# The first half product of a block as seven quarter products, worked in during the block before

## Chip, core and metric

The kernel runs on one core of one Trainium2 chip. The metric is the device time of one launch in microseconds (us); the time before is the median of three runs. Below, PE is TensorE, DVE is VectorE, ACT is ScalarE, POOL is GpSimd, SP is the engine that here only issues DMAs. "PEld" rows are PE's weight loads.

## What is computed

Input x is 32 images of 14 x 14 x 512 in fp32. Two layers follow. The first is by far the larger: a group norm, then 18 blocks, each a 512 x 512 product with bias and gelu. After blocks 1, 4 and 9 the activation is kept as an anchor; after blocks 11, 14 and 17 (the targets) a small network on the pooled activation makes gates, and a gated sum of the three anchors is added. The second layer is a group norm and a grouped 3 x 3 convolution. Cut to what matters here:

```python
for i in range(NUM_BLOCKS):
    nx = jax.nn.gelu(jnp.einsum('bhwc,cd->bhwd', x, block_w[i]) + block_b[i])
    if i in TARGET_IDX:
        ...
        nx = nx + gammas[t] * routed
    x = nx
    if i in ANCHOR_IDX:
        anchors.append(x)
```

## The kernel before

**Tiles.** The 32 images go in 8 pairs of tiles; a tile is two images, N = 392 pixels, with channels on the 128 partitions. A step is one block of one pair: a product of the 512 x 512 weights with 512 channels x 784 pixels, in fp32. There are 18 x 8 = 144 steps and one gap; `steps` (L99 to L110) lists them. Mostly runs of 3 or 6 blocks of one pair alternate with runs of the neighbouring pair.

**Seven half products.** A step would be eight half products (256 x 256 weights with 256 channels x 392 pixels), in a 2 x 2 scheme over channel halves and the two tiles. The kernel does Winograd's form of Strassen's scheme: seven half products on sums of weights (`sums`, s0 to s3, L398) and on sums of activations (`pre_adds`, t0 to t3, L440). The weight sums are worked out for the first pair and kept in DRAM (skeep); later pairs load them. One half product is 2 output halves d x 2 K halves = four matmuls of 128 x 128 weights with 392 columns (`part`, L480, does one d: two matmuls); an fp32 matmul leaves two records in the trace.

**One of the seven once more.** The product of s0 and t0 (accumulators Z) is itself done by seven quarter products, each one matmul with 196 columns (`inner`, L532). They need four weight sums u (`inner_sums`, L419) and four activation sums v (end of `pre_adds`, L453 to L460), and between them small copies of quarters of Z by ACT (L548, L549, L554, L563) and one add on DVE (L569, "the add of f").

**Order in a step** (`block`, L462; seven ticks, NP7 = 7, at which `run(tick)` lets out other work):

- X = a11 q00, each half copied to Y by ACT (`save`, L543)
- first quarter matmuls of Z; tick 0
- Y0 += a12 q10 with d = 0, two quarter matmuls of Z, Y1 += a12 q10 with d = 1; gelu of Y gives output quarter (0,0); tick 1
- X0 += s1 t1, copied to c2; two quarter matmuls of Z; tick 2
- X1 += s1 t1, copied to c2; the last quarter matmul of Z and the add of f; Z copied to c3; tick 3
- X += s2 t2; DVE adds X to c3; gelu gives quarter (1,1); tick 4
- Z += s3 q11; DVE adds Z to c2 (L523); gelu gives quarter (0,1); tick 5
- t0 and the four v of the next step on DVE (L586); X += a22 t3; gelu gives quarter (1,0); tick 6; then t1, t2, t3 of the next step (L592).

Here q00, q01, q10, q11 are the four quarters of the step's input (first index: channel half; second: tile), and X0, X1 the two accumulators of X. t0 is q01 - q00 of the next input, so that it needs both the gelu of Z and that of Y where the next step is of the same pair. Where the next step belongs to the other pair, its input has long been there.

Every engine works its instructions in the order of the program. PSUM has six banks for X, Y, Z and the convolution's sums (L79).

**Planner.** All other work (gates, norms, loads, building the convolution's weights, the convolution's units) is put into ticks by `put` (L130), against a budget of us for DVE and ACT in each tick (`ROOM`, L117). Weight loads (`load_block`, L386) come one step ahead (L1409), the sums' loads at ticks 3 to 5 (L1412), all on SP. The convolution's units (`plan_unit`, L1097) may stand at ticks 1 to 4 (`fits`, L1094).

Of the kernel before, what the change touches and what calls it, by code (L numbers as in the profile page):

```python
# [20 lines left out]
def kernel(  # L21
# [51 lines left out]
    qpool = ctx.enter_context(tc.tile_pool(name="qpool", bufs=38))  # L73
# [43 lines left out]
    ROOM = {"dve": (3.3, 1.9, 1.4, 1.8, 1.4, 0.6, 0.0), "act": (1.5, 0.75, 0.75, 0.8, 1.5, 1.5, 1.5)}  # L117
# [239 lines left out]
    def plan_start(p):  # L357

        t0 = NP7 * at_step[p, 0]
        parts = [(2 * p + n, c) for n in range(2) for c in range(NCK)]  # L360
        NIN = 3
        a = t0 - LEAD
        at(a - 30, copy_in, p)
        turned = []
        b = 0
        for j, (t, c) in enumerate(parts):
            at(t0 - LEAD - 6 if j < NIN else turned[j - NIN], load_blocks, t, c)
            turned.append(put(max(a, turned[j - NIN] + 4 if j >= NIN else 0), {"dve": 0.45 + c % NH * 0.15}, turn_blocks, t, c))
            a = turned[j]
        for j, (t, c) in enumerate(parts):  # L370
            b = max(b, put(turned[j // NH * NH + NH - 1], {"dve": 0.7}, stats_in, t, c))
        b = put(b + 1, {"dve": 0.8}, lambda: whole(scales_mean(pst[p])))
        b = put(b + 1, {"dve": 0.2}, lambda: whole(scales_rstd(pst[p])))
        b = put(b + 2, {"dve": 0.8}, lambda: scales_newton(pst[p]))
        e = b
        for c in range(NCK):
            e = max(e, put(b, {"dve": 1.6}, norm_in, p, c))
        b = e

        assert b < t0 - 1  # L380
        at(t0 - 2, take_start, p)
# [3 lines left out]

    def load_block(k):  # L386
        w = wpool.tile([P, NCK, C], F32, tag="w", name=f"w_{k}")
        nc.sync.dma_start(w, block_w[steps[k][1]].rearrange("(k p) d -> p k d", p=P))
        D = C // 2
        wts[k] = dict(  # L390
            a11=w[:, :NH, :D], a12=w[:, NH:, :D], a21=w[:, :NH, D:], a22=w[:, NH:, D:], s={}
        )
# [24 lines left out]
    ukeep = [tc.dram_tile([P, 4 * P], F32, name=f"ukeep{i}") for i in range(NB)]  # L417

    def inner_sums(k):  # L419

        p, i = steps[k]
        d = wts[k]
        u = d["u"] = spool.tile([P, 4, P], F32, tag="u", name=f"u_{k}")
        if p > 0:
            nc.sync.dma_start(u.rearrange("p j d -> p (j d)"), ukeep[i])
            return
        a = corners(d["s"][0], P)
        for j, (i0, i1) in enumerate((  # L430
            (a[1][0], a[0][0]), (a[1][1], u[:, 0]), (a[1][1], a[1][0]), (a[0][1], u[:, 1]),
        )):
            nc.vector.tensor_tensor(u[:, j], i0, i1, ALU.subtract)  # L433
        nc.sync.dma_start(ukeep[i], u.rearrange("p j d -> p (j d)"))
# [5 lines left out]
    def pre_adds(p, q, name, js):  # L440


        t = ts.setdefault(p, {})
        for j in js:
            t[j] = quarter(f"t{j}_{name}")
            i0, i1 = [
                lambda: (q[0][1], q[0][0]),
                lambda: (q[1][1], t[0]),
                lambda: (q[1][1], q[0][1]),
                lambda: (q[1][0], t[1]),  # L450
            ][j]()
            nc.vector.tensor_tensor(t[j], i0, i1, ALU.subtract)  # L452
            if j == 0:  # L453
                v = t["v"] = quarter(f"v_{name}").rearrange("p k (n x) -> p (k n) x", x=HW)
                b = corners(t[0], HW)
                for l, (i0, i1, op) in enumerate((
                    (b[1][0], b[1][1], ALU.add), (v[:, 0], b[0][0], ALU.subtract),
                    (b[0][0], b[1][0], ALU.subtract), (b[0][1], v[:, 1], ALU.subtract),
                )):
                    nc.vector.tensor_tensor(v[:, l], i0, i1, op)  # L460

    def block(k):  # L462
# [17 lines left out]
        def part(acc, d, lhsT, rhs, first=False):  # L480
            for kk in range(NH):
                nc.tensor.matmul(  # L482
                    acc[d][:, :N], lhsT=lhsT[:, kk, d * P : (d + 1) * P],
                    rhs=rhs[:, kk, :], start=first and kk == 0, stop=kk == NH - 1,
                    skip_group_check=True,
                )
# [5 lines left out]
        def gelu(half, n, srcs):  # L492
            o = quarter(f"o{half}{n}_{name}")
            dst[half][n] = o
            for d in range(NH):
# [17 lines left out]

        def temps(j):
            return [tmp.tile([P, N], F32, tag="c", name=f"c{j}{d}_{name}") for d in range(NH)]
# [8 lines left out]


        a, b, u, v = corners(s[0], P), corners(t[0], HW), w["u"], t["v"]
        Z = []

        def corner(d, n):
            return Z[d][:, n * HW : (n + 1) * HW]  # L530

        def inner(d, n, lhsT, rhs, first=False):  # L532
            nc.tensor.matmul(  # L533
                corner(d, n), lhsT=lhsT, rhs=rhs, start=first, stop=True, skip_group_check=True
            )

        X = bank("x")
        Y = bank("y")  # L540
        for d in range(NH):
            part(X, d, w["a11"], q[0][0], True)
            save(Y, X, (d,))  # L543
        Z += bank("z")
        inner(1, 0, u[:, 0], v[:, 0], True)
        inner(1, 1, a[0][0], b[0][0])
        f = tmp.tile([P, N], F32, tag="c", name=f"f_{name}")[:, :HW]
        nc.scalar.copy(f, corner(1, 0))  # L548
        nc.scalar.copy(corner(0, 0), corner(1, 1))  # L549
        run(tick)  # L550
        part(Y, 0, w["a12"], q[1][0])
        inner(0, 0, a[0][1], b[0][1])
        inner(1, 1, u[:, 1], v[:, 1])
        nc.scalar.copy(corner(1, 0), corner(1, 1))  # L554
        part(Y, 1, w["a12"], q[1][0])
        gelu(0, 0, [Y[d][:, :N] for d in range(NH)])
        run(tick + 1)
# [3 lines left out]
        inner(1, 0, a[1][1], v[:, 3])  # L561
        inner(1, 1, u[:, 2], v[:, 2])
        nc.scalar.copy(corner(0, 1), corner(1, 1))  # L563
        run(tick + 2)
        part(X, 1, s[1], t[1])
        save(c2, X, (1,))
        inner(0, 1, u[:, 3], b[1][1])
        both = Z[1][:, :N].rearrange("p (n x) -> p n x", n=2)
        nc.vector.tensor_tensor(  # L569
            both, both, f.unsqueeze(1).to_broadcast([P, 2, HW]), ALU.add  # L570
        )
        c3 = temps(3)
        save(c3, Z)
        run(tick + 3)
        product(X, s[2], t[2])
        add(c3, X)
        gelu(1, 1, c3)
        run(tick + 4)
        product(Z, s[3], q[1][1])
        add(c2, Z)  # L580
        gelu(0, 1, c2)
        run(tick + 5)
        pn = steps[k + 1][0] if k + 1 < len(steps) and steps[k + 1][1] != GAP else None
        if pn is not None:
            qn = dst if pn == p else cur[pn]
            pre_adds(pn, qn, f"{k + 1}", (0,))  # L586
        product(X, w["a22"], t[3])
        gelu(1, 0, [X[d][:, :N] for d in range(NH)])
        cur[p] = dst
        run(tick + 6)  # L590
        if pn is not None:
            pre_adds(pn, qn, f"{k + 1}", (1, 2, 3))  # L592
# [9 lines left out]
    def load_gates(k):  # L602
        ti = TARGETS.index(steps[k][1])
        w1 = fpool.tile([P, NCK, HID], F32, tag="w1", name=f"w1_{k}")
        nc.sync.dma_start(w1, fc1_w[ti].rearrange("(k p) h -> p k h", p=P))
        w2 = fpool.tile([HID, NA * C], F32, tag="w2", name=f"w2_{k}")
        if steps[k][0] == 0:
            nc.sync.dma_start(w2, fc2_w[ti])
        else:
            nc.sync.dma_start(w2[:, C:], w2keep[ti])  # L610
        fcw[k] = w1, w2
# [3 lines left out]
    def gate_differences(k, t):  # L615


        w2 = fcw[k][1]
        for a in range(1, NA):
            nc.vector.tensor_tensor(  # L620
                w2[:, a * C : (a + 1) * C], w2[:, a * C : (a + 1) * C], w2[:, :C], ALU.subtract
            )
        nc.sync.dma_start(w2keep[t], w2[:, C:])
# [7 lines left out]
    def gate_hidden(k, t, name, box):  # L631
        w1, _ = fcw[k]
# [14 lines left out]
    def gate_logits(k, name, box):  # L647
        _, w2 = fcw.pop(k)
        h = box["h"]
        lps = box["l"] = aux(f"lps_{name}")  # L650
        for m in range(NCK, NL):
            nc.tensor.matmul(  # L652
                lps[:, m * NB4 : (m + 1) * NB4], lhsT=w2[:, m * P : (m + 1) * P], rhs=h,
# [440 lines left out]
    def fits(tick):  # L1094
        return steps[tick // NP7][1] == GAP or 1 <= tick % NP7 <= 4

    def plan_unit(m, u, tk, ahead, stay=False):  # L1097
# [12 lines left out]
        assert b // NP7 == a // NP7  # L1110
# [283 lines left out]
    pre_adds(0, cur[0], "0", range(4))  # L1394
    inner_sums(0)
    for j in range(2, 4):
        sums(0, j)

# [3 lines left out]
    for k in range(len(steps)):  # L1402
# [5 lines left out]
        if k > 0:  # L1408
            at(NP7 * (k - 1), load_block, k)  # L1409
            if p > 0:  # L1410
                at(NP7 * (k - 1) + 3, inner_sums, k)
            for tk, j in ((3, 0), (3, 1), (4, 2), (5, 3)):  # L1412
                at(NP7 * (k - 1) + tk, sums, k, j)
            if p == 0:
                at(NP7 * (k - 1) + 4, inner_sums, k)
                for tk, us in ((3, 0.5), (4, 0.0), (5, 0.0)):
                    left["dve"][NP7 * (k - 1) + tk] = us
        if i in TARGETS:
            at(NP7 * (k - 1 if k == len(steps) - 1 else k) + 4, load_gates, k)
            for tk, us in enumerate((1.2, 0.0, 0.3, 0.8, 0.3, 0.2, 0.0)):  # L1420
# [5 lines left out]
    for p in range(NPAIR):  # L1426
        plan_differences(p)
        for i in TARGETS[:-1]:
            a = plan_gates(p, i, plan_head(p, i), [[0, 1], [2, 3]])
            assert a < NP7 * at_step[p, i + 1] - 1, (p, i, a, NP7 * at_step[p, i + 1])  # L1430
# [54 lines left out]
```

## Time and profile before

| | |
|---|---|
| median of three runs | 2910.55 us (2909.18 to 2910.66) |
| the profiled execution | 2908.12 us |
| its span, first to last instruction | 2906.4 us, 33728 instructions |
| mean granted PE clock | 0.994 |
| PE matmul records of line L482 (392 columns) | 48 in each step |
| PE matmul records of line L533 (196 columns) | 14 in each step |
| L533 matmul z<-v,u: busy, mean of one | 215.0 us, 331 ns |
| L482 matmul x<-t,s: busy, mean of one | 833.3 us, 494 ns |
| L460, the v: mean of one | 354 to 362 ns |
| L569, the add of f: mean of one | 572 ns |
| L548, L549, L554, L563, the small copies: mean of one | 323, 328, 307, 307 ns |
| L519, copy of a whole accumulator: mean of one | 469 to 497 ns |
| DMA | 507.35 MB, mean 175 GB/s |

How to read it: matmuls are pipelined, and the length of a record holds the way through the array; so the mean of one is longer than the distance between two in a stream. A row of the timeline gives the start, the time from the first start to the last end, engine, line, operation, output and input, shape and count; in brackets the idle time before it and what ended it. A row of the groups also gives the idle time in front of all its instructions.

### The profile page before, as it was taken

The page shows a single profiled execution, that of the slowest core. Times are in us where ns is not written, and L with a number is a line of the kernel's source. Part 1 is how long each engine was busy: PE and PEld are TensorE (multiplying, and loading weights), DVE is VectorE, ACT ScalarE, POOL GpSimd, SP SyncE. Part 2 cuts the span into 40 slices and gives each one's busy share as a digit, 9 for nine tenths or more (in the row PEclk, how much of TensorE's full clock was granted, in tenths as well). Part 3 has the DMA queues.
Part 4 walks back from the last instruction along what each step waited for, and adds up shares of the span by engine and source line. Part 5 has one row for each costly group of instructions (what it writes and reads, how often), then busy time and mean ns, then how long its engine had stood idle before and what let it go on. Part 6 is the DMA issues. An engine that isn't in the chain of part 4 may idle for free.

```text
span 2906.4 us, 33728 instructions
## 1 busy us (share of the span) xinstructions
PE 2867.1 (99%) x10545; PEld 1889.0 (65%) x10545; DVE 1932.9 (67%) x3996; ACT 1548.5 (53%) x3865; POOL 78.7 (3%) x59
## 2 busy tenths in 40 slices
PE   8999999999999999999999999999999999999987
PEld 5666666666666666666666666666666666666667
DVE  6888878765487565774657746676466764655775
ACT  4445555555556454564545645555455554655551
POOL 0000000000000000000000000000000000000000
PEclk9999999999999999999999999999999999999999
DMA  5544566644575566664666656756567753453676
GB/s 190 181 156 160 177 198 190 187 148 158 160 196 154 164 192 175 200 171 141 209 178 179 179 162 180 202 173 187 160 183 202 183 165 130 136 174 120 195 223 162
DMA packets 494053, 507.35 MB, mean 175 GB/s; under 512 B 242915, under 2 KB 303922, under 8 KB 493874
## 3 DMA queue, kind: packets, MB, share of 16 engines
q1 hardware_dynamic: 478378, 487.12, 56.1%
q0 software_dynamic: 4608, 12.85, 2.4%
q10 hardware_dynamic: 10888, 5.22, 0.7%
q8 instruction: 85, 1.39, 0.2%
q14 instruction: 94, 0.77, 0.1%
HBM read 421.32 MB, written 94.99 MB: 178 GB/s over the span
## 4 chain that ended last, share of the span: by engine, by line
PE 94%; DMA 3%; DVE 2%; ACT 0%; SPq 0%; issue 0%; DVEq 0%; ACTq 0%
PE x L482 51%; PE y L482 13%; PE z L482 13%; PE z L533 11%; PE cps L1013 4%; PE lps L652 1%; DMA x<-x2d 1%; DMA xkeep<-xt 1%; PE hps L635 1%; DMA w<-in_L_conv_fc_w_dram 0%; DMA s<-skeep 0%; DVE x L1002 0%; DMA xin<-in_x_dram 0%; DMA bq<-band 0%; DVE t L452 0%
## 5 line engine op out<-in xcount | busy, mean ns | idle before, releaser
L482 PE MATMUL x<-t,s 128*128 128x392 f32 x2304 | 833.3, 494 | 0.3 <-ACT c L519 0.3
L482 PEld LDWEIGHTS x<-t,s 128*128 128x128 f32 x2304 | 427.5, 190 | 230.3 <-ACT c L519 0.9
L499 ACT ACTIVATE o<-c,bias 128x392 f32<-128x392 f32 x480 | 291.8, 619 | 352.9 <-DVE c L523 352.9
L482 PE MATMUL x<-t,w 128*128 128x392 f32 x1152 | 403.2, 493 | 0.0
L482 PE MATMUL y<-o,w 128*128 128x392 f32 x1088 | 402.6, 492 | 0.0
L482 PE MATMUL x<-o,w 128*128 128x392 f32 x1088 | 380.8, 493 | 0.0
L482 PE MATMUL z<-o,s 128*128 128x392 f32 x1088 | 380.8, 493 | 0.0
L523 DVE TENSOR_TENSOR c<-x,c 128x392 f32<-128x392 f32 x288 | 160.7, 565 | 265.8 <-PE x L482 192.8
L482 PEld LDWEIGHTS x<-t,w 128*128 128x128 f32 x1152 | 218.4, 190 | 158.7
L482 PEld LDWEIGHTS z<-o,s 128*128 128x128 f32 x1088 | 206.3, 190 | 149.7
L482 PEld LDWEIGHTS x<-o,w 128*128 128x128 f32 x1088 | 206.2, 190 | 149.5
L519 ACT COPY c<-x 128x392 f32<-128x392 f32 x288 | 140.0, 486 | 299.9 <-PE x L482 299.9
L452 DVE TENSOR_TENSOR t<-o,o 128x784 f32<-128x784 f32 x272 | 263.9, 970 | 51.1 <-ACT o L499 49.0
L569 DVE TENSOR_TENSOR z<-z,f 128x392 f32<-128x392 f32 x144 | 82.3, 572 | 314.1 <-ACT z L563 313.9
L452 DVE TENSOR_TENSOR t<-o,t 128x784 f32<-128x784 f32 x272 | 262.9, 966 | 0.8 <-PE x L482 0.7
L482 PEld LDWEIGHTS y<-o,w 128*128 128x128 f32 x1088 | 200.1, 190 | 75.9 <-ACT y L519 0.2
L523 DVE TENSOR_TENSOR c<-z,c 128x392 f32<-128x392 f32 x288 | 161.5, 563 | 111.5 <-PE z L482 110.9
L519 ACT COPY y<-x 128x392 f32<-128x392 f32 x288 | 133.6, 469 | 175.0 <-PE x L482 173.7
L533 PE MATMUL z<-v,u 128*128 128x196 f32 x864 | 215.0, 331 | 7.8 <-DVE u L433 4.5
L533 PEld LDWEIGHTS z<-v,u 128*128 128x128 f32 x864 | 157.1, 191 | 49.6 <-issue 10.6
L499 ACT ACTIVATE o<-x,bias 128x392 f32<-128x392 f32 x240 | 137.6, 582 | 63.6 <-PE x L482 55.7
L499 ACT ACTIVATE o<-y,bias 128x392 f32<-128x392 f32 x240 | 141.4, 590 | 53.1 <-PE y L482 53.1
(139 smaller groups left out, 3181.6 us busy)
## 6 DMA issues: line engine op xcount, KB each, us to landing
w<-in_L_conv_block_w_dram SPq DMA_DIRECT2D x144, 1024.0 KB
s<-skeep SPq DMA_DIRECT2D x504, 256.0 KB
u<-ukeep SPq DMA_DIRECT2D x126, 256.0 KB
x2d<-xc SPq DMA_DIRECT2D x116, 224.0 KB
x<-x2d SPq DMA_DIRECT2D x104, 224.0 KB
skeep<-s SPq DMA_DIRECT2D x72, 256.0 KB
xkeep<-xt SPq DMA_DIRECT2D x32, 392.0 KB
o<-xkeep POOLq DMA_DIRECT2D x32, 392.0 KB, 8.1
```

What stands on the lines that cost most here:

```text
L452: nc.vector.tensor_tensor(t[j], i0, i1, ALU.subtract)
L482: nc.tensor.matmul(acc[d][:, :N], lhsT=lhsT[:, kk, d * P : (d + 1) * P], rhs=rhs[:, kk, :], start=first and kk == 0, stop=kk == NH - 1, sk ...
L499: nc.scalar.activation(o[:, d, :], srcs[d], AF.Gelu_apprx_tanh, bias=bias[:, r : r + 1])
L519: nc.scalar.copy(cs[d][:, :N], acc[d][:, :N])
L523: nc.vector.tensor_tensor(cs[d], acc[d][:, :N], cs[d], ALU.add)
L533: nc.tensor.matmul(corner(d, n), lhsT=lhsT, rhs=rhs, start=first, stop=True, skip_group_check=True)
L569: nc.vector.tensor_tensor(both, both, f.unsqueeze(1).to_broadcast([P, 2, HW]), ALU.add)
L635: nc.tensor.matmul(hps[:, :NB4], lhsT=w1[:, kk, :], rhs=box["pooled"][:, kk, :], start=(kk == 0), stop=(kk == NCK - 1),)
L652: nc.tensor.matmul(lps[:, m * NB4 : (m + 1) * NB4], lhsT=w2[:, m * P : (m + 1) * P], rhs=h, start=True, stop=True,)
L1013: nc.tensor.matmul(pv[:, :, lo:hi], lhsT=bw[:, g, dy], rhs=xv[:, :, lo + dy - 1 : hi + dy - 1], start=g == 0 and j == 0, stop=j == 2, skip ...
```

## The change

- `ahead(k)` says for which steps the first product X is done in the step before: pairs other than the first, not block 0, not the block after a target, and one step left out.
- For these, X is done by seven quarter products (the same scheme as Z, now a class `Inner` in four parts), with their own weight sums u1 of a11 and their own v of q00. The u1 are worked out by DVE in the first pair's steps and kept in DRAM; later they are loaded into the place of a21 in the weight tile, which isn't needed there.
- Its parts stand among the half products of the step before: part 0 after s2 t2, part 1 within s3 q11, part 2 before a22 t3, part 3 within it. Then ACT copies the new X to the new Y.
- In every step, ahead or not: Y comes in one piece after X (or first of all), by K halves; Z's quarter products start after it; s2 t2 stands half before and half after Z's last quarter product; t0 and the v of the next step are queued in the tick before a22 t3 rather than after.
- Weights come in two or three DMAs for all pairs but the first, one tick earlier; the sums' loads move by one tick; the budgets `ROOM` are new, with more where the next step isn't ahead; the convolution's units may stand at ticks 0 and 1 only; the start does t0, then u, then t1, two weight sums, t2 and t3; the first third of the gate weights has its own tile.

The core of the diff:

```diff
-    ROOM = {"dve": (3.3, 1.9, 1.4, 1.8, 1.4, 0.6, 0.0), "act": (1.5, 0.75, 0.75, 0.8, 1.5, 1.5, 1.5)}
+    ROOM = {"dve": (2.1, 0.8, 2.2, 2.6, 0.5, 0.0, 0.0), "act": (0.4, 0.6, 1.0, 1.5, 0.75, 0.0, 1.5)}
...
+    def ahead(k):
...
+        p, i = steps[k]
+        if (p, i) == (NPAIR - 2, TARGETS[1] + 2):
+            return False
+        return p > 0 and i not in (GAP, 0) and i - 1 not in TARGETS
...
+            nc.sync.dma_start(a11, src[:, :NH, :D])
+            if ahead(k):
+                nc.sync.dma_start(a21, ukeep[i][1].rearrange("p (k d) -> p k d", k=NH))
+            nc.sync.dma_start(w[:, NH:], src[:, NH:])
...
+        def part(self, j):
+            a, b, u, v, at = self.a, self.b, self.u, self.v, self.corner
+            if j == 0:
+                self.mm(1, 0, u[0], v[:, 0], True)
+                self.mm(1, 1, a[0][0], b[0][0])
+                nc.scalar.copy(at(0, 0), at(1, 1))
+                self.f = tmp.tile([P, N], F32, tag="c", name=f"f_{self.name}")[:, :HW]
+                nc.scalar.copy(self.f, at(1, 0))
+            elif j == 1:
+                self.mm(0, 0, a[0][1], b[0][1])
+                self.mm(1, 1, u[1], v[:, 1])
+                nc.scalar.copy(at(1, 0), at(1, 1))
+            elif j == 2:
+                self.mm(1, 0, a[1][1], v[:, 3])
+                self.mm(1, 1, u[2], v[:, 2])
+                nc.scalar.copy(at(0, 1), at(1, 1))
+            else:
+                self.mm(0, 1, u[3], b[1][1])
+                both = self.acc[1][:, :N].rearrange("p (n x) -> p n x", n=2)
+                nc.vector.tensor_tensor(
+                    both, both, self.f.unsqueeze(1).to_broadcast([P, 2, HW]), ALU.add
+                )
...
+        if ahead(k):
+            X, Y = first.pop(k)
+        else:
+            X, Y = bank("x"), bank("y")
+            for d in range(NH):
+                part(X, d, w["a11"], q[0][0], True)
+                save(Y, X, (d,))
+        for kk in range(NH):
+            for d in range(NH):
+                part(Y, d, w["a12"], q[1][0], kks=(kk,))
+        gelu(0, 0, flat(Y))
         run(tick)
...
+        inner.part(2)
+        part(X, 0, s[2], t[2])
+        inner.part(3)
         c3 = temps(3)
         save(c3, Z)
...
+        part(X, 1, s[2], t[2])
         add(c3, X)
         gelu(1, 1, c3)
...
+        if kn and ahead(kn):
+            XN, wn = bank("x"), wts[kn]
+            inner = Inner(XN, wn["a11"], wn["u1"], qn[0][0], vn, f"x{kn}")
+            inner.part(0)
+        run(tick + 3)
+        part(Z, 0, s[3], q[1][1])
+        if kn and ahead(kn):
+            inner.part(1)
+        part(Z, 1, s[3], q[1][1])
         add(c2, Z)
         gelu(0, 1, c2)
+        run(tick + 4)
+        if kn:
+            qn = dst if pn == p else cur[pn]
+            pre_adds(pn, qn, f"{kn}", (0,))
+            if ahead(kn):
+                inner.part(2)
+        part(X, 0, w["a22"], t[3])
+        gelu(1, 0, flat(X), (0,))
+        if kn and ahead(kn):
+            inner.part(3)
+            YN = bank("y")
+            save(YN, XN)
+            first[kn] = XN, YN
         run(tick + 5)
...
+        part(X, 1, w["a22"], t[3])
+        gelu(1, 0, flat(X), (1,))
         cur[p] = dst
         run(tick + 6)
...
+        if kn:
+            pre_adds(pn, qn, f"{kn}", (1, 2, 3))
...
     def fits(tick):
-        return steps[tick // NP7][1] == GAP or 1 <= tick % NP7 <= 4
+        return steps[tick // NP7][1] == GAP or tick % NP7 <= 1
...
+    pre_adds(0, cur[0], "0", (0,))
+    inner_sums(0, 0)
+    pre_adds(0, cur[0], "0", (1,))
     for j in range(2, 4):
         sums(0, j)
+    pre_adds(0, cur[0], "0", (2, 3))
```

## The prediction

> **What bounds the kernel now.** I read the page's busy times and its chain of work first, then the timeline of one step on TensorE (PE), then the same stretch on all engines.
>
> ```profile
> PE 2867.1 (99%) x10545; PEld 1889.0 (65%) x10545; DVE 1932.9 (67%) x3996; ACT 1548.5 (53%) x3865; POOL 78.7 (3%) x59
> ...
> PE 94%; DMA 3%; DVE 2%; ACT 0%; SPq 0%; issue 0%; DVEq 0%; ACTq 0%
> ```
>
> PE holds 94% of the chain that ended last. Is it full, or only called busy? One whole step, PE alone:
>
> ```profile
> 1407.73 2.80 PE L482 MATMUL x<-o,w 128*128 128x392 f32 x8
> 1410.36 0.49 PE L533 MATMUL z<-v,u 128*128 128x196 f32 x2
> 1410.69 0.49 PE L533 MATMUL z<-t,s 128*128 128x196 f32 x2
> 1411.02 1.48 PE L482 MATMUL y<-o,w 128*128 128x392 f32 x4
> ...
> 1420.58 2.80 PE L482 MATMUL z<-o,s 128*128 128x392 f32 x8
> 1423.22 2.80 PE L482 MATMUL x<-t,w 128*128 128x392 f32 x8
> 1425.85 0.49 PE L482 MATMUL x<-o,w 128*128 128x392 f32 x1
> ```
>
> Read starts against starts, since the lengths overlap. Each fp32 matmul leaves two records. Eight records of 392 columns take 1423.22 to 1425.85 = 2.63, so 0.329 each; four of 196 columns take 1410.36 to 1411.02, so 0.1655 each. A step has 48 of the first and 14 of the second: 15.80 + 2.32 = 18.12, and the step is 1425.85 - 1407.73 = 18.12. Nothing is lost between instructions. So a PE record removed is worth its full time, if nothing arrives later than PE does now; and each new wait of PE is paid in full.
>
> **Removed and added on PE.** A half product is 8 x 0.329 = 2.63; seven quarter products are 14 x 0.1655 = 2.32. The change saves 0.316 in each step whose first product is done ahead. The condition (pair over 0, not block 0, not after a target, one exception) holds in 104 of the 144 steps, by the list of steps: at most 104 x 0.316 = 33 us.
>
> A rule speaks against this. The Trainium skill, "TensorE: Matmul & The Clock Gate", section "Back-to-back issue gap", says that in a real stream each matmul's spacing is set by its weight load too, and gives 81 ns at 128 columns where streaming alone takes 56. As an estimate from that page, 25 ns more on each quarter record gives 14 x 0.19 = 2.66: the saving is gone. But the row has four quarter records in a run, each with its own load, at 0.1655, just what half the columns should take, and the new order never puts more than four in a run. I take the row.
>
> **The new wait.** After the last Z product ends (call it E) the new order on PE is: two quarter matmuls of the next X, half of w22 (X0), one quarter matmul, the other half (X1), then at once the next step's Y0, Y1 (first K half), Y0, Y1 (second). Y1 accumulates on a copy of the finished next X1, and that X1 needs the add of f (now L569), which the code places in VectorE's (DVE's) queue behind t0 and its four v. t0 waits for the last gelu of Z. What that chain costs, the trace shows:
>
> ```profile
> 1423.22 2.80 PE L482 MATMUL x<-t,w 128*128 128x392 f32 x8
> 1423.42 0.56 DVE L523 TENSOR_TENSOR c<-z,c 128x392 f32<-128x392 f32 x1 [0.57 <-PE z L482]
> 1424.02 0.62 ACT L499 ACTIVATE o<-c,bias 128x392 f32<-128x392 f32 x1 [0.52 <-DVE c L523]
> 1424.67 0.98 DVE L452 TENSOR_TENSOR t<-o,o 128x784 f32<-128x784 f32 x1 [0.69 <-ACT o L499]
> ...
> 1426.63 0.36 DVE L460 TENSOR_TENSOR v<-t,v 128x196 f32<-128x196 f32 x1
> 1426.90 0.97 DVE L452 TENSOR_TENSOR t<-o,t 128x784 f32<-128x784 f32 x1
> 1427.42 0.47 ACT L519 COPY y<-x 128x392 f32<-128x392 f32 x1
> ...
> 1428.74 0.47 ACT L519 COPY y<-x 128x392 f32<-128x392 f32 x1 [0.85 <-PE x L482]
> ```
>
> E is 1423.22. The next DVE instruction after the fourth v starts at 1426.90, E + 3.68; over the steps of one pair it is between 3.41 and 3.84, mostly 3.69, even in steps where DVE has little else. There the add of f will stand: + 0.57 (mean of L569) + 0.03 (DVE to ACT: 1423.98 to 1424.02) + 0.47 (the copy) + 0.05 to PE = E + 4.81. PE wants Y1 at E + 0.66 + 1.32 + 0.33 + 1.32 + 0.66 = E + 4.29. It waits 0.52. A wait also costs the restart:
>
> ```profile
> 2756.79 0.46 ACT L519 COPY c<-x 128x392 f32<-128x392 f32 x1
> ...
> 2757.31 1.25 PE L482 MATMUL x<-t,s 128*128 128x392 f32 x3 [0.31 <-ACT c L519]
> ```
>
> Here PE starts 0.05 after the copy's end, and the three records take 1.25, where three in a stream take 1.15: 0.10 more, the second weight load laid bare. So 0.62 a step against 0.316 saved: +0.30. PE's queue is in order, so all of the next step stands behind Y1. On ACT the gelu of X1 stands behind the waiting copy; it ends at 4.76 + 0.03 + 0.59 = E + 5.38, and the third Y matmul that needs it comes at 4.81 + 0.76 = E + 5.57: covered. ACT work planned into that tick (0.75) would delay the one quarter matmul instead, by about as much; that wait takes the place of this one, it does not add to it.
>
> 90 of the 104 steps follow a step of their own pair: 90 x 0.30 = +27. The 14 others follow another pair's step, where t0 waits for no gelu: the same gap is 2.91 there, the copy is done at E + 4.03, and PE doesn't wait. Their predecessors are target steps with a longer gelu (two halves and reads), for which I take 0.1 back: 14 x -0.2 = -3.
>
> **The new order in the other 40 steps.** X, Y now follow each other without the quarter matmuls between. The second copy above ends at 1429.21, 3.36 after the step's start (1425.85), so Y1 can go at 3.41; PE is there at 2.63 + 0.66 = 3.29. 0.12 + 0.10 restart, in 38 of them: +8. More is possible when ACT has planned work at that place (new budget 1.5 or 2.1 us), nothing below zero; bounds 0 and +20.
>
> **The start.** The first step takes 25.7 (19.11 to 44.80), 7.6 over the others: PE waits 4.54 for u (L433), then runs its next records at half speed. Now Y stands ahead of Z, and u ahead of t1 to t3 (2.66 of DVE work), so u comes at about 24.4, before Y can end (25.1, after 0.7 of waiting for copies). Bounds -7 and 0; I take -5.
>
> **DMAs and SP.** The weight load becomes three issues (two where not ahead) of about 0.4 each on SP and goes a tick earlier; the bytes are the same or 256 KB fewer. Its a11 and a21 are now needed some 10 us after issue, where w had 18. PE's only larger waits in mid-run are for u and s (at 807, 1530 and 2238 us, 3.4 together with restarts), with about the same lead; these two now have 2.6 more, so that I take -3. A late w (a xkeep load of 392 KB lands 8.1 after issue) could cost the 7 pair starts 2 each: 0 to +14; I take 0. The sums' issue at tick 3 waits on the same products as before. w2's split is 3 DMAs in all: nothing.
>
> **DVE and ACT load.** Each ahead step adds four v (1.22) and one add (0.57) on DVE, four small copies (4 x 0.32) on ACT: 104 x 1.8 = 187 makes DVE 2120 of some 2940 (72%), ACT 1548 + 132. The planner's DVE budget falls from 10.4 to 8.2 a step, so a full step needs 9.9 + 8.2 = 18.1, by nominal lengths, and has 18.4. Conv taps move to ticks 0 and 1, with their own PE time unchanged. That fits with nothing to spare; the full steps (over a third) may lose 0.1 each: +5, bounds 0 and +30.
>
> Sum: 27 - 3 + 8 - 5 - 3 + 5 = +29 on the profiled 2908.1 (span 2906.4): 2937. That execution lies 2.4 below the median of the runs, so the forecast for the median is 2940.
>
> **Rivals.**
> 1. The wait isn't there (faster). If the add of f ran before t0, or PE came to Y1 0.52 later for free, the 104 steps would give -33: 2910.6 - 33 + 8 - 5 - 3 + 5 = 2883. It decides at E + 4.29 for the copy. For it: only 0.52 is missing. Against it: the code's order, and 3.41 as the shortest gap seen, which still misses by 0.24 before the restart. 13%.
> 2. Part of the wait is covered, so that saving and wait cancel: at 0.24 + 0.10 for all 90 steps, 90 x 0.02, total 2910.6 + 2 - 3 + 2 = 2912. 7% around no change.
> 3. DVE becomes the bound in full steps: 60 of them longer by 0.5 instead of 0.1 add 25 more: 2965 and up. For it: no spare time above. Against: before, steps with 18 us of DVE work in 18.12 made no PE wait. 12%.
> 4. The change does less than it says: the condition is met in 104 steps by the list, so this is only the 40 steps above.
>
> **Chances.** The forecast 68% (2922 to 2962 by its own bounds), rival 3 12%, rival 2 7%, rival 1 13%. The 80% range, 2912 to 2966, takes in the upper part of rival 2 and the start of 3. Faster by over 0.2% (about what a measurement of this kernel can tell from no change) 14%, within it 6%, slower 80%.
>
> **What would show it.** Right: on PE a wait in front of the y<-o,w records, released by ACT's copy y<-x, near 0.5 in some 90 steps; steps of 18.4 within a pair and 17.8 to 18 after another pair; the add of f starting right after the fourth v; the first step near 20. Wrong: Y records that follow X without a gap (rival 1); quarter records spaced at 0.19 (the rule); DVE over 85% (rival 3).

## The result, and the profile after

The changed kernel takes 2974.63 us (median of four runs, 2968.39 to 2978.09) against 2909.86 for the kernel before on the same chip. The ratio is 1.0222, with a 95% interval of 1.0203 to 1.0242: it is slower, by 65 us where 29 were forecast, and it lies above the range. The profiled execution took 2978.09, its span is 2976.4, so the two spans compared below differ by 70.0.

The page of the changed kernel, busy times and the chain that ended last:

```profile
PE 2884.2 (97%) x11169; PEld 1954.6 (66%) x11169; DVE 2120.0 (71%) x4576; ACT 1653.5 (56%) x4281; POOL 75.8 (3%) x59
...
PE 10%; DVE 3%; DMA 2%; ACT 1%; SPq 0%; issue 0%; POOL 0%; DVEq 0%; ACTq 0%; POOLq 0%
```

PE's busy time rose by 17 although the first product got shorter: a record's length holds the way through the array, so part of each wait behind it counts as busy. The chain is traced back over a sixth of the span only, so it can't be read as a share any more; DVE stands at the 2120 that the prediction worked out.

One step's end and the beginning of the next in the changed kernel, PE alone (start, length, engine, line, operation, output and input, shape, count, idle time before and what ended it):

```profile
548.99 0.83 PE L507 MATMUL x<-v_x,w 128*128 128x196 f32 x4
549.65 1.48 PE L557 MATMUL x<-t,w 128*128 128x392 f32 x4
550.97 0.49 PE L507 MATMUL x<-o,w 128*128 128x196 f32 x2
551.30 1.48 PE L557 MATMUL x<-t,w 128*128 128x392 f32 x4
552.61 0.82 PE L557 MATMUL y<-o,w 128*128 128x392 f32 x2
553.80 2.24 PE L557 MATMUL y<-o,w 128*128 128x392 f32 x6 [0.36 <-ACT y L598]
555.88 0.49 PE L507 MATMUL z<-v,u 128*128 128x196 f32 x2
...
568.09 1.48 PE L557 MATMUL x<-t,w 128*128 128x392 f32 x4
```

E, the end of Z, is 548.99. The four quarter records take 0.66, so 0.165 each. The first two Y records start at 552.61 and should be followed at 553.27; the next ones start at 553.80, 0.53 later, and the six take 555.88 - 553.80 = 2.08 where six in a stream take 1.975: 0.10 for the restart. The step is 568.09 - 549.65 = 18.44, against 18.12 before. The bracket shows only 0.36 of the wait, since the record before it still counts as running for the rest: starts have to be read against starts.

The same stretch on the other two engines:

```profile
550.44 0.97 DVE L491 TENSOR_TENSOR t<-o,o 128x784 f32<-128x784 f32 x1 [0.42 <-ACT o L575]
...
552.40 0.36 DVE L473 TENSOR_TENSOR v<-t,v 128x196 f32<-128x196 f32 x1
552.67 0.57 DVE L531 TENSOR_TENSOR x<-x,f_x 128x392 f32<-128x392 f32 x1
553.28 0.47 ACT L598 COPY y<-x 128x392 f32<-128x392 f32 x1 [1.14 <-DVE x L531]
553.66 0.59 ACT L575 ACTIVATE o<-x,bias 128x392 f32<-128x392 f32 x1
```

The add of f (L531) starts right after the fourth v, at E + 3.68, and the copy ends at E + 4.76: both as worked out. So this part of the forecast is seen as it was drawn.

Where the 70.0 lie, summed over PE's records (a stand is the distance between two starts less the length in a stream; a step is cut at the first record of a22 t3):

| part | predicted | measured |
|---|---|---|
| start, to the first a22 t3 | -5 | -6.4 |
| 90 steps done ahead after a step of their pair: stands at Y and at the last quarter product 65.3 (before 0.7), less 90 x 0.316 | +27 | +36.2 |
| 14 after the other pair: 2.6 - 14 x 0.316 | -3 | -1.8 |
| 38 steps not done ahead: X to Y | +8 | +11.3 |
| all other stands (loads of s, u, w1; small copies): 32.5, before 14.1 | -3 | +18.4 |
| DVE and ACT too full | +5 | see below |
| after the last a22 t3: 112.3, before 101.6 | 0 | +10.7 |
| rest | | +1.6 |

Two lines stand out that were put down at or below nothing: the other stands, and the end. The longest of PE's waits in the changed kernel show both:

```profile
PE x L507 <- ACT x L527: 18.0, 41, 1.1
PE y L557 <- ACT y L598: 16.9, 49, 0.4
PE cps L1095 <- DMA x<-x2d: 14.9, 3, 12.1
PE hps L717 <- DMA w<-in_L_conv_fc_w_dram: 6.0, 4, 3.7
PE x L557 <- DMA s<-skeep: 4.5, 5, 1.3
```

(Sum, times, longest.) The first two rows are the step's end: in 41 steps ACT's planned work in tick 4 stands in front of the copy that the last quarter product needs, in most of the 49 others the add of f in front of Y1. The third row is the end. The last two are loads: w1, the gates' first weights, and s. They come in the steps that follow a pair's last target and in the step after the gap; these seven steps hold 22.7 of stands, where they held 5.2 before.

### The profile page after: what moved, and what is told of

Its sections match the earlier page's. It is cut to its first block, busy times and chain, and to the rows that moved or that the text cites. A ratio compares the mean times of both kernels' runs of the same rounds, so it can differ in the third digit from the quotient of the medians.

```text
span 2976.4 us, 36085 instructions
## 1 busy us (share of the span) xinstructions
PE 2884.2 (97%) x11169; PEld 1954.6 (66%) x11169; DVE 2120.0 (71%) x4576; ACT 1653.5 (56%) x4281; POOL 75.8 (3%) x59
## 5 line engine op out<-in xcount | busy, mean ns | idle before, releaser
L557 PE MATMUL x<-t,s 128*128 128x392 f32 x2304 | 853.0, 493 | 5.5 <-DMA s<-skeep 4.5
L557 PE MATMUL y<-o,w 128*128 128x392 f32 x1088 | 404.3, 504 | 18.7 <-ACT y L598 16.9
L557 PE MATMUL x<-t,w 128*128 128x392 f32 x1152 | 420.0, 492 | 0.0
L557 PE MATMUL z<-o,s 128*128 128x392 f32 x1088 | 397.9, 494 | 0.0
L575 ACT ACTIVATE o<-c,bias 128x392 f32<-128x392 f32 x480 | 292.9, 620 | 187.3 <-DVE c L602 182.2
L598 ACT COPY c<-z 128x392 f32<-128x392 f32 x288 | 126.2, 489 | 174.1 <-PE z L507 170.6
L531 DVE TENSOR_TENSOR z<-z,f_z 128x392 f32<-128x392 f32 x144 | 82.6, 573 | 195.4 <-ACT z L527 195.4
L575 ACT ACTIVATE o<-y,bias 128x392 f32<-128x392 f32 x240 | 139.9, 586 | 114.2 <-PE y L557 107.2
L507 PE MATMUL x<-v_x,w 128*128 128x196 f32 x832 | 189.1, 329 | 1.7 <-DMA w<-ukeep 1.7
L507 PEld LDWEIGHTS x<-v_x,w 128*128 128x128 f32 x832 | 150.3, 190 | 60.6 <-issue 2.9
L507 PE MATMUL x<-o,w 128*128 128x196 f32 x624 | 162.1, 341 | 18.0 <-ACT x L527 18.0
```

What stands on the lines that cost most here:

```text
L507: nc.tensor.matmul(self.corner(d, n), lhsT=lhsT, rhs=rhs, start=first, stop=True, skip_group_check=True,)
L531: nc.vector.tensor_tensor(both, both, self.f.unsqueeze(1).to_broadcast([P, 2, HW]), ALU.add)
L557: nc.tensor.matmul(acc[d][:, :N], lhsT=lhsT[:, kk, d * P : (d + 1) * P], rhs=rhs[:, kk, :], start=first and kk == 0, stop=kk == NH - 1, sk ...
L575: nc.scalar.activation(o[:, d, :], srcs[d], AF.Gelu_apprx_tanh, bias=bias[:, r : r + 1])
L598: nc.scalar.copy(cs[d][:, :N], acc[d][:, :N])
```

## Experiments

The theory after the first look: T1, the step's end costs what the queue "t0, four v, add of f" costs, as predicted; and the rest comes from loads and the end of the kernel. Rivals: ACT's planned work, the new order itself, DVE too full. All kernels do the whole computation. Ratios are to the kernel before on the same chip, with 95% intervals; its median there was 2909.5 to 2911.0 us, so that the times may be compared with each other. Counts of stands are from each run's one profiled execution.

### e1, e2 and both: what holds the step's end

e1 queues the add of f ahead of t0 and the v; e2 takes ACT's planned work out of tick 4; the third does both.

```diff
-            pre_adds(pn, qn, f"{kn}", (0,))
             if ahead(kn):
                 inner.part(2)
+            else:
+                pre_adds(pn, qn, f"{kn}", (0,))
...
             inner.part(3)
+            pre_adds(pn, qn, f"{kn}", (0,))
```

```diff
-"act": (0.4, 0.6, 1.0, 1.5, 0.75, 0.0, 1.5)
+"act": (0.4, 0.6, 1.0, 1.5, 0.0, 0.75, 1.5)
```

> The add of f of the first half product is queued on DVE ahead of t0 and the sums v of the next step, instead of behind them; nothing else is changed, the work is the same. Theory (the wait at the step's end is this queue: t0 and v 5 operations, then the add, then the copy Y1, then TensorE's first matmul into Y1): about 50 to 57 of the 90 same-pair steps with the plain wait of 0.62 us lose 0.5 of it, so 2974.6 - 27 = about 2947 us, and in the other some 35 steps the wait at the last quarter product (0.41 to 1.3 us, behind ACT's planned work) stays as it is. First rival (what is lost comes from loads that land late and from the end of the kernel): under 5 us of change, about 2972 us. Second rival (DVE is simply too full at the end of a step, whatever the order): the wait moves to the next step's first small products, which need v, and 2965 to 2975 us result.

> Only the planner's room changes: ACT's 0.75 us for planned work in tick 4 (just ahead of the copy that the last quarter product of the next X waits for) goes to tick 5, behind the copies into Y. Theory: the 35 to 41 steps whose wait is at the last quarter product become steps with the plain wait of 0.62 us; their stalls add up to 65.3 - 90 x 0.62 = about 9 us more than that, so 2974.6 - 9 = about 2966 us, or less gain if the work moved to tick 5 delays the GELU of X1. Rival (ACT's planned work is not the cause of those waits): no change, 2972 to 2977 us.

> Both edits: the add of f ahead of t0 and v on DVE, and ACT's tick 4 empty. Theory (the two queues are one chain's two halves): with both out of the way the stalls at the end of the 90 same-pair steps, 65 us in all, fall to restarts of at most 0.1 to 0.2 us each, so -47 to -60 us: 2915 to 2928 us. Rival (they are independent, each with its own steps): the sum of the two single gains, -27 - 9: about 2938 us. Rival (loads and end): over 2965 us.

Measured: e1 2939.8 us (1.0101, 1.0081 to 1.0121), 35 less than the changed kernel, where about 27 were expected. The stands at the end of the 90 steps fall from 65.3 to 31.3: T1 holds. e2 3001.0 us (1.0309, 1.0285 to 1.0332): 26 more, where 9 less were expected. Both 2925.6 us (1.0053, 1.0036 to 1.0069), within what was expected; the same stands are 5.3.

Why e2 alone went the other way is seen in its trace, at the end of one step, on DVE, ACT and PE:

```profile
1467.84 0.57 DVE L531 TENSOR_TENSOR x<-x,f_x 128x392 f32<-128x392 f32 x1
...
1468.44 0.47 ACT L598 COPY y<-x 128x392 f32<-128x392 f32 x1 [1.13 <-DVE x L531]
...
1468.82 0.81 ACT L819 ACTIVATE gq<-o,g 128x196 f32<-128x196 f32 x2
...
1468.96 0.93 PE L557 MATMUL y<-o,w 128*128 128x392 f32 x2 [0.36 <-ACT y L598]
...
1469.53 0.57 ACT L575 ACTIVATE o<-x,bias 128x392 f32<-128x392 f32 x1
```

The moved work (L819) now stands behind the copy that waits for the add of f, and in front of X1's gelu (L575), which the second half of Y needs. PE stands a second time, 0.43 + 0.10, in the steps that have such work: "PE y <- ACT o" is 11.1 us in 41 steps, a wait that the changed kernel doesn't list. The expectation had named this danger and given it no number. With f first the copy isn't late, the same work fits behind it, and nothing stands. It also shows what the ACT work in tick 4 cost in the changed kernel: little, since Y1 would have been late anyway; the two waits took each other's place in most steps (total 0.62 to 0.65 either way; more in 20 of the 90: 0.79 in 13, and 1.04 to 1.5 in seven, six of them after block 0 of a pair). It costs only once the other is gone: e1 keeps 31 us of it.

### e3: the new order without the first product done ahead

```diff
-        return p > 0 and i not in (GAP, 0) and i - 1 not in TARGETS
+        return False
```

> No step's first product is done ahead: the first product is the half products of before in every step, with the new order within a step, the new loads and the new room. The ukeep copies of a21 and the small sums go with it. Theory (the new order costs 0.22 us at X -> Y in each of 143 steps = 31 us, the start gains 6, and the late loads and the end, about 13 + 11 + 8, belong to the new order and calendar): 2909.9 + 31 - 6 + 32 = about 2967 us. Rival (the late loads and the longer end come from the quarter products: their loads of a21, their DVE sums): 2909.9 + 31 - 6 = about 2935 us.

Measured: 3008.1 us (1.0332, 1.0313 to 1.0351), 41 above the higher expectation. So with the seven quarter products the kernel is 33.5 us faster than without them; all of the loss and more is in what came with them. The 33.5 isn't their saving alone: without them the 65 at the steps' ends are gone as well, X to Y costs 54 (0.22 and more in 142 steps) where it cost 11, and the other stands are some 19 longer. By luck these cancel nearly: all stands from the first to the last a22 t3 are 107 in e3 and 112 in the changed kernel. The steps after the other pair's last target stand 38 in e3, with u up to 4.2 late. In one of them SP issues u 5.7 after the a22 t3, behind twelve small loads xb, four xr and a unit's loads. Late loads therefore don't come from the quarter products' own bytes: e3 moves 474 MB, the changed kernel 506, and e3 waits longer.

### e5 to e8: three single causes on top of e1 and e2

Each is an edit of the kernel with both edits (2925.6 us): the gate weights loaded three ticks earlier; the column copies of the last pair but one at their old ticks; Z's first two small products between X and Y again where the step isn't done ahead; and all together.

```diff
-            at(NP7 * (k - 1 if k == len(steps) - 1 else k) + 4, load_gates, k)
+            at(NP7 * (k - 1 if k == len(steps) - 1 else k) + (4 if p == 0 else 1), load_gates, k)
```

```diff
-                a = put(a, {"act": 0.6}, columns, p, c, n, d, 0)
-            at(a, store_columns, p, c, d, 0)
+                if p == NPAIR - 2:
+                    at(a, columns, p, c, n, d, 0)
+                else:
+                    a = put(a, {"act": 0.6}, columns, p, c, n, d, 0)
+            at(a + (p == NPAIR - 2), store_columns, p, c, d, 0)
+            a += p == NPAIR - 2
```

```diff
                 save(Y, X, (d,))
+            Z = bank("z")
+            inner = Inner(Z, s[0], w["u0"], t[0], t["v"], f"z{name}")
+            inner.part(0)
```

> On the kernel with both edits (2925.6 us): only the loads of the gate weights w1 and w2 are issued three ticks earlier, at tick 1 of the target's step instead of tick 4, for pairs after the first. Theory (in the six steps that follow a pair's last target TensorE stands for w1, u and s, 24 us in all[...]; w1 is late because it is issued behind u, three s and a unit's loads): two of those steps lose 7 us each, the step after the gap 2.5 us: about 2909 us. Rival (the transfers as a whole are late there, whatever comes first: w1 goes early and s and u take its place): 2920 to 2928 us.

> On the kernel with both edits (2925.6 us): only the column copies of the last pair but one are planned two to a tick right behind their gates, as the planner had them before the change, and not where its smaller room lets them slip to the end of the last step. Theory (the part behind the last step is 8 to 10 us longer than before because the stores of these columns stand in SP's queue ahead of the loads of the tail): 2925.6 - 8 = about 2917.5 us. Rival (the tail is longer for another reason, such as its own loads of the bands and stores of the output): no change, 2923 to 2928 us.

> On the kernel with both edits (2925.6 us): in the 38 steps whose first product is not done ahead, Z's first two small products go between X and Y again. Theory (there Y's first product waits 0.12 us for the copy and restarts in 0.10): 30 steps lose 0.22 and five 0.5, and the start stays: 2925.6 - 9 = about 2916.5 us; if the start loses its gain of 6 us (the first step then needs u and v early, as before), about 2922 us. Rival (the wait moves to the small products' own copies): no change, 2923 to 2928 us.

> All five edits together. If they are independent, 2925.6 - 16 - 8 - 9 = about 2893 us, faster than the kernel before (2910); if the start loses its gain, about 2899. If the late loads only change places, about 2909. All under the rival that the late loads, the tail and the order are no causes: 2920 us or more.

Measured: e5 2930.3 us (1.0073, 1.0056 to 1.0091), no gain: the stands after the last targets go from 24.2 to 33.8, now for u and s, so the rival holds. e6 2921.5 (1.0041, 1.0025 to 1.0056): its interval overlaps that of the kernel it is built on, and in its profile the end takes 110.2 against 109.5: the columns' slip isn't what makes the end longer. e7 2918.4 (1.0025, 1.0013 to 1.0038): X to Y falls from 11.4 to 0.7 in the 38 steps, and the start keeps most of its gain (the first a22 t3 at 36.5, against 35.6); as expected, less 3 us of small waits that take its place. e8 2931.2 (1.0067, 1.0052 to 1.0081), far from the 2893 of independent causes: the early gate loads spoil it (stands after the last targets 32.6). What is issued first only decides what comes late.

### e9 to e12: the queue itself

On e7's kernel (the e12 of this section is e12_all_fixes): xb and xr, the small loads for a later pair's start, issued from POOL's queue; s1 ahead of u; the columns' old ticks with eight output stores moved to POOL's queue; and all three.

```diff
-            nc.sync.dma_start(
+            nc.gpsimd.dma_start(
                 xs[q * TB : (q + 1) * TB],
...
```

```diff
-            for tk, j in ((3, 0), (3, 1), (3, 2), (4, 3)):
+            for tk, j in ((3, 0), (3, 1), (3, 2), (4, 3)) if p == 0 else ((2, 1), (3, 0), (3, 2), (4, 3)):
```

```diff
-                    at(b + 1 + v, store_out, m, c, v, q, nc.sync)
+                    at(b + 1 + v, store_out, m, c, v, q, nc.gpsimd if m == NBAT - 2 else nc.sync)
```

> On the kernel of the two edits and the order of the steps not done ahead (2918.4 us): the small loads of a later pair's start (xb and xr, twelve to a block of 128 channels) are issued from POOL's queue instead of SP's. Theory (the late u, s and w1 in the steps after a pair's last target stand behind these loads in SP's queue, and the new order needs s1 over 4 us sooner after the step's start): most of the 19.5 us in those steps goes, about 2903 us. Rival (the bytes in flight, not the queue's order, make them late): 2915 us and more, and the stands only change places. Second rival (POOL issues such loads slowly[...]): above 2918 us.

> On the same kernel (2918.4 us): the load of s1 is planned at tick 2, behind the last product that reads the old s1, ahead of the load of u, which SP holds until the last small product of Z. Theory (s1's deadline in a step done ahead came forward, while its load stayed behind u in the queue): the waits for s in front of X's first s1 part go, and u and w1 come no later: -4 to -6 us, about 2913 us. Rival (the transfers' total counts): no change, 2916 to 2921 us.

> On the same kernel (2918.4 us): the columns of the last pair but one at their old ticks, and the eight output stores of the units done in the gap, which the new calendar brings into the last two steps of SP's queue (two times 3.6 us of issuing), issued from POOL. Theory (the part behind the last step is longer because SP comes to the tail's loads late, behind these stores): it falls from 108 to 102 us, about 2912 us. Rival (the tail is set by its own transfers): no change, 2916 to 2921 us.

> These three sets of edits together, on the same kernel. Theory: 2918.4 - 15 - 2 - 6 = about 2895 us, below the kernel before (2910.4). Rival (transfers' total): 2912 us and more.

Measured: e9 2895.7 us (0.9956, 0.9943 to 0.9970), 22.7 less than e7 and 7 below what was expected: below the kernel before. e10 2922.4 (1.0040, 1.0025 to 1.0054), no gain. e11 2917.0 (1.0027, 1.0018 to 1.0036), no gain: the end takes 109.0. e12, all three, 2894.8 (0.9949, 0.9931 to 0.9967), as e9.

### e13 and e14: is that queue a part of the change's loss?

The same edit alone, on the kernel before and on the changed kernel.

> The kernel before the change, with only xb and xr issued from POOL's queue. Theory (its order needs u, s and w1 later, and so it stands only some 3 us for them in the steps after a pair's last target): 2907 to 2910 us, at most 3 us faster. Rival (the queue was a cost before the change as well, and what the edit gains is no part of the change's loss): about 2887 to 2895 us.

> The changed kernel with only xb and xr issued from POOL's queue. Theory: the steps after a pair's last target stand 13.5 us for loads in the changed kernel's profile, of which some 2 are the copy's wait that stays: 2974.6 - 12 = about 2963 us, less than on the faster kernel, where the loads have less time. Rival (equal share whatever the speed): -23, about 2952 us.

Measured: e13 2908.4 us (0.9993, 0.9986 to 1.0001): nothing to gain there. e14 2955.3 (1.0157, 1.0141 to 1.0173), 19.3 less than the changed kernel, between the two expectations. So this queue is a cost of the change alone, about 19 of its 65 us. In the profiled executions, which lie 26.9 apart, the other stands fall by 20, to what they were before the change, and the end by 6.3. One step after a pair's last target shows how. In the kernel before, SP's issues:

```profile
1857.40 1.88 SPq L282 DMA_DIRECT2D xr<-xcol  x4
1859.38 0.37 SPq L427 DMA_DIRECT2D u<-ukeep  x1
1859.80 0.91 SPq L406 DMA_DIRECT2D s<-skeep  x2
```

and on PE the first a22 t3 and the next step's first s1 t1:

```profile
1858.42 2.80 PE L482 MATMUL x<-t,w 128*128 128x392 f32 x8
1861.06 2.80 PE L482 MATMUL x<-o,w 128*128 128x392 f32 x8
1863.69 0.49 PE L533 MATMUL z<-v,u 128*128 128x196 f32 x2
...
1867.65 0.95 PE L635 MATMUL hps<-pool,w 128*128 128x4 f32 x8
1868.46 1.56 PE L482 MATMUL x<-t,s 128*128 128x392 f32 x4
```

The same step in the changed kernel, SP:

```profile
1882.53 6.91 SPq L275 DMA_DIRECT2D xb<-xcol  x8
1889.49 1.88 SPq L282 DMA_DIRECT2D xr<-xcol  x4
1891.46 1.91 SPq L275 DMA_DIRECT2D xb<-xcol  x4
1893.47 0.41 SPq L450 DMA_DIRECT2D u<-ukeep  x1
1893.93 1.39 SPq L427 DMA_DIRECT2D s<-skeep  x3
```

and PE:

```profile
1891.52 1.48 PE L557 MATMUL x<-t,w 128*128 128x392 f32 x4
...
1894.68 2.80 PE L557 MATMUL y<-o,w 128*128 128x392 f32 x8
1897.31 0.49 PE L507 MATMUL z<-v,u 128*128 128x196 f32 x2
1897.64 0.49 PE L507 MATMUL z<-t,s 128*128 128x196 f32 x2
1899.41 1.55 PE L557 MATMUL x<-t,s 128*128 128x392 f32 x4 [1.27 <-DMA s<-skeep]
```

Count from the first record of a22 t3. Before, u and two s are issued from 0.96 to 2.29, and the first s1 t1 runs at 10.04. After, u goes out at 1.95 and the last of three s at 3.80, and the first s1 t1 could run at 1897.97, that is 6.45: X, 2.63 long, is no longer done here, and half of Z's small products and the gates' products (hps) now come later. The need came 3.6 nearer and the issue went 1 to 1.5 later; it stands for 1.44. With xb and xr on POOL's queue (e14) the three s have all gone out 4.3 ahead of that record, and nothing stands.

### e15: the gate loads again

> The kernel with all fixes (2894.8 us), and w1 and w2 issued three ticks earlier again, for pairs after the first. Theory (with SP's queue free of the small loads there is room to bring w1 forward without making u and s late): the 3.7 us in the step after the gap and the 3.3 us in one other step go, with the slow records after them: about 2887 us. Rival (u and s take w1's place as before): 2893 to 2899 us.

Measured: 2887.2 us (0.9923, 0.9909 to 0.9937), the fastest version, 22 below the kernel before. That this comes from the gate loads isn't shown: the profiled span is that of e12_all_fixes (2890.7 and 2890.3). In the step after the gap w1's stand of 3.5 has gone, while Z's first small product stands 5.9 where it stood 3.9. The profile names no releaser for it; it is no late load, since u was issued 18.7 ahead, and the first of the v on DVE ends at 2726.93, 0.10 before that product starts.

## Why the prediction was wrong

**Right, with its number.** The saving: quarter records stand at 0.165, which makes 33 in 104 steps; that e3 gave 33.5 is luck, as said there. The surcharge of the Trainium skill ("TensorE: Matmul & The Clock Gate", section "Back-to-back issue gap") isn't seen in four fp32 records in a run. The wait at Y1 and its restart: 0.52 + 0.10 in the 43 steps that show it plainly, a step of 18.44. The 38 steps not done ahead: 0.22 in 30 of them, 11.3 in all with a few of 0.46. The start: -6.4. DVE as the bound (rival 3): DVE at 71%, and its load stays at 2116 in the kernel with both edits, where the stands at the steps' ends are gone, so it wasn't the bound.

**Wrong: "DMAs and SP".** The step said that the late u and s "now have 2.6 more" and took -3; it measured +18.4. It looked at a transfer's way from issue to landing in a common step. Its 2.6 is what Y in front of Z gives where X is still done in the step itself. In a step done ahead X's 2.63 is gone as well: in the step above, u is first needed at 5.27 before and 5.79 after, 0.5 more and not 2.6, and s1 is needed 3.6 sooner, which the step didn't count. Nor did it lay SP's queue of the steps after a pair's last target beside the new deadlines of s1, s2 and w1, where the xb and xr loads stand in front; the kernel before already issues them there, with room to spare that no wait shows. The upper bound of "+14" was given to the late w at pair starts, which didn't come. e13 and e14 put the queue's share at 19, of which a part lies at the end.

**Wrong in size: the 90 steps.** 0.62 was right for a step with nothing else in ACT's tick 4; the mean is 0.73. "That wait takes the place of this one, it does not add to it" holds for 70 of them, not for the 20 named above: +9.

**Missed: the end.** It was left out of the sum as unchanged. It is 10.7 longer in the changed kernel. Half of that is one wait: PE stands 12.3 for the tail's loads x<-x2d, 7.3 before. The row of the kernel before that answers to the third one above:

```profile
PE cps L1013 <- DMA x<-x2d: 9.6, 3, 7.1
```

These loads are issued 22.5 after the last a22 t3, 13.9 before; six stores of columns, 11.4 of issuing, stand in front of them, two stores before. That the smaller ACT room lets the last columns slip was a reason that fell (e6), so did the output stores in SP's queue (e11). It is 6.3 shorter in e14, and e13, whose end has the order of the kernel before, takes 105.1 against 101.6. So 3.5 of the 10.7 may be the spread of single executions. What sets the end stays open, with 4 to 11 us.

**The packing term** (+5) has nothing left to explain beyond the rest of 1.6. One sum is off, without weight: rival 2 carries +2 where the four terms it stands for (8, -5, -3, 5) make +5, so it should read 2915.

So the sign came from the right mechanism, and the size missed because nearly a third of the loss lay in a queue that was priced at below nothing.

## What to carry to other kernels

When work is moved within a step, write down for every load that the step uses when it is issued and when it is now first needed, in the steps where the issuing queue is fullest and not in a common one: a load that never showed a wait may have had a few us of room, and the change may spend them. If moving loads within one in-order queue only changes which of them is late, move the bulk that needs no hurry to another queue, and run that edit on the old kernel too, to see whose cost it was. And two waits that hide each other have to be removed together: here one edit alone gained 35, the other lost 26, both gained 49.

## What the hardware showed unexpectedly

A stand of PE can cost more than its length. In the kernel with both edits PE waits 4.9 for w1; the stretches around it (us, busy times of PE, weight loads, DVE, ACT and POOL with counts, granted clock, DMA share, GB/s):

```profile
1516.00:1521.00 5.00, 0.24 (x1) 0.00 (x0) 3.89 (x9) 0.49 (x1) 0.00 (x0) 0.90 1.07 268
1521.00:1527.00 6.00, 5.87 (x17) 4.65 (x18) 0.00 (x0) 0.57 (x2) 0.00 (x0) 0.52 0.76 230
1527.00:1530.00 3.00, 3.00 (x14) 2.17 (x13) 0.67 (x2) 1.41 (x4) 0.00 (x0) 1.00 1.00 324
```

For six us after it the granted clock is 0.52 and records are twice as far apart, which costs some 3 us on top. In e7 a stand of 1.0 was followed, after 0.9 us of products of four columns, by 3.7 us of such records (1152.9 to 1156.6; half clock from 1153.15 to 1156.56), while the stands of 1.29 at the first steps of each pair in the changed kernel were followed by none. The Trainium skill ("TensorE: Matmul & The Clock Gate", section "Part 1: The HAM clock gate") has the clock decided over free-running windows of 3.4 us, and the traces agree. In all 17 of them the granted clock changes only at points of a grid of 3.41 us, and each stretch at half clock that ends inside the span lasts a multiple of 3.41.

They also show what decides. Take each record at its length in a stream at full clock, in proportion to its columns (0.329 for 392), and add up what falls into each window of 3.41. Of the windows at full clock, the 143 that were followed by half clock hold at most 1.36 us of such work, and none of the 14165 followed by full clock holds less than 1.25. The limit, an estimate from these, is about 1.3. In e7 the window from 1149.7 to 1153.1 holds 1.25, since products of four columns count for next to nothing; a stand of 1.29 and its restarts among full products leave some 1.9.
